# A Mamba-style vision block: one state's product with C on GpSimd in unit 10, and six issue places shifted

## The chip, the core and the metric

The kernel runs on one core of a Trainium2 chip. The metric is the device time of one execution in microseconds (us). The engines are named as in the profile: PE (matrix products; PEld is its weight load), DVE (VectorE), ACT (ScalarE), POOL (GpSimd) and SP, whose queue issues the DMAs.

## What is computed

Two images of 96 channels and 128 x 128 pixels pass through two layers. The first layer's mixer is four selective scans (rows, rows reversed, columns, columns reversed) over 16,384 positions. Each has 192 inner channels and 16 states:

```python
xc = silu(conv(xc) + conv_b)                       # causal, 4 taps
dt_raw, Bm, Cm = split(xc @ xproj_w.T)             # 6, 16, 16
dt = softplus(dt_raw @ dt_w.T + dt_b)
def step(h, t):
    dt_t, u_t, B_t, C_t = t
    dA = exp(dt_t[:, :, None] * A)
    h = dA * h + dt_t[:, :, None] * B_t[:, None, :] * u_t[:, :, None]
    y = einsum('bds,bs->bd', h, C_t)
    return (h, y)
y = (scan(step) + Dp * xc) * silu(z)
out = y @ outp_w.T
```

The four results are fused by one matrix and added to the input. After it come a normalised feed-forward network with quantised products, a 3 x 3 convolution in the second layer and another such network.

## The kernel before

For each image `normalize` makes the normalised input, `mamba` does the four scans, and `ffn_and_conv` does the rest. The change is in `mamba`, which takes most of the time.

`mamba` runs 64 **steps** for an image: 2 pairs of directions (row and column direction side by side on the 128 partitions, the second pair reversed) times 32 tiles of T = 512 positions. For two images that is 128 steps. The 2 x 192 channels of a pair make three groups g of 128 partitions. A step has 24 **units**, `units = [(g, s) ...]`, s = 0, 2, ... 14: a unit is two states of one group. Unit 8g + s/2 is (g, s), so unit 10 is (1, 4).

For a unit the work goes through the engines thus:

- SP loads the B row and the C row of four states, broadcast over partitions (`row_tile`, L346, tiles `row0` and `row1`, 1 MB each, 5 and 4 buffers). One such tile serves two units.
- POOL multiplies the B rows of two units by dt x u (`b_part`, L350) and adds the carried state into the first column (L354; L353 once for each group).
- ACT makes the decays exp(dt x A) into the PSUM tile `da` (`decay`, two L360 for a unit, 3 buffers).
- DVE scans the two states (`scan`, L364). In most units the result overwrites `da`. In the six units in `BY_POOL` (units 0, 4, 8, 12, 16, 20) it overwrites the B row tile instead.
- The product with C (h x c into the C row tile) is done by DVE (L459), or for the six units by POOL (`by_pool`, L371).
- ACT copies the last column of the state (L460) to `hst`, for the next step.
- PE sums the products over the states into the PSUM tile `y` with an identity matrix (`sums`, L368), starting each group from Dp x xc (L465). After a group's 8 units DVE multiplies y by the gate (`gated`, L375).

The order in each engine's queue is the order of the Python calls, written out by hand (`in_order`); nothing reorders it. The loop at the end of `mamba` goes over units k. At even k it issues B products for units k + 2 and k + 3. Then come `issue(k, 0)`, the first scan of unit k, `behind(k - 1)` (product with C, copy and sums of the unit before), the decay of unit k + 2, the second scan, `issue(k, 1)`. Where unit k - 1 is the first of a group, `behind` comes after the second scan. A POOL product of unit k is issued at (k + 1, 1), its sums at (k + 3, 1).

`issue(k, where)` hands out what `later` has put down for that unit. Besides the POOL products this is the preparation of the **next** step, `prologue`, whose list `at` holds (unit, where, function): `conv` and `conv_out` (the four taps on PE, evicted by ACT), `silu` of xc and of the gate sz (L270, with a load of the function table ahead, and L271, the load of the table for exp behind), `gate` and `gate_out` (PE, and the eviction by ACT, L258), `mix` (two DMAs that reorder rows of group 1), `rows` and `rows_out` (the projections), `rows_to_dram`, `dt_in` and `dt_out` (PE L295, ACT L300), `softplus` (L304, L305) and `dt_u` (POOL L309), `entry`. Units 24 and up are units of the step that uses the results: 27 is its unit 3. All matmul results of the preparation share one PSUM buffer, `misc`.

Of the kernel before, what the change touches and what calls it, by code (L numbers as in the profile page):

```python
# [15 lines left out]
ALU = mybir.AluOpType  # L16
# [7 lines left out]
T = 512  # L24
# [10 lines left out]
ROW_BUFS = (5, 4)  # L35
AHEAD = 2
BY_POOL = tuple((g, s) for g in range(3) for s in (0, 8))
BCO = 32
SEG = 8
NBC = 4 * S  # L40
# [3 lines left out]
def tile_metaformer(ctx: ExitStack, tc: tile.TileContext, a: dict, out: bass.AP):  # L44
    nc = tc.nc
# [5 lines left out]
    def const(name, shape):  # L51
        t = cpool.tile(list(shape), F32, name=name)
        nc.sync.dma_start(t, a[name])
        return t
# [20 lines left out]
    convb = const("convb", (128, 2, NG))  # L75
    bcw = const("bcw", (128, 2, NG, BCO + NBC))
    dtw = const("dtw", (2 * RK, 2, NG * 128))
# [113 lines left out]
    def mamba(acc, xnr, xnc, pools, heads):  # L191

        with ExitStack() as st:
            pool = lambda n, bufs, **kw: st.enter_context(tc.tile_pool(name=n, bufs=bufs, **kw))
# [6 lines left out]
            hst = one.tile([128, NG, S], F32, name="hst")  # L201
# [19 lines left out]
            def prologue(pi, i, d):  # L221

                rev = pi == 1
                first = pi == 0 and i == 0
                queue = nc.scalar if first else nc.sync
                lo = L - (i + 1) * T if rev else i * T
# [46 lines left out]
                def rows():  # L273

                    d["ps"] = misc()
                    for g in range(NG):
                        nc.tensor.matmul(  # L277
                            d["ps"][0 : BCO + NBC, :], bcw[:, pi, g, :], d["xc"][:, g, :], start=g == 0, stop=g == NG - 1
                        )

                def rows_out():
                    d["rows"] = one.tile([BCO + NBC, T], F32, name="rows")
                    nc.scalar.copy(d["rows"], d["ps"][0 : BCO + NBC, :])

                def rows_to_dram():

                    d["bcd"] = rows_d.tile([2, S // 4, 2, 4, T], F32, name="bcd")
                    queue.dma_start(d["bcd"].rearrange("k q d s t -> (k q d s) t"), d["rows"][BCO:, :])

# [25 lines left out]

                at = [(-3, 1, load), (3, 0, partial(mix, "xc")), (11, 0, partial(silu, "xc"))]
                at += [(25 if first else 9, 0, partial(mix, "sz")), (31, 1, partial(silu, "sz"))]
                at += [(12, 0, rows), (13, 1, rows_out), (14, 0, rows_to_dram)]  # L320
                for g, k in ((1, 1), (0, 5), (2, 9)):
                    at += [(k, 0, partial(conv, g)), (k + 1, 1, partial(conv_out, g))]
                gates = ((1, 24, 24, 1), (0, 27, 27, 1), (2, 28, 28, 1)) if first else ((1, 7, 8, 0), (0, 18, 19, 0), (2, 21, 22, 0))
                for g, k, o, where in gates:
                    at += [(k, 0, partial(gate, g)), (o, where, partial(gate_out, g))]
                soft = ((0, 1, 16), (1, 3, 26)) if first else ((0, 3, 17),)
                for x0, x1, k in soft:
                    at += [(k, 1, partial(softplus, x0, x1))]
                for g, k in enumerate((14, 24, 25) if first else (14, 15, 16)):
                    at += [(k, 0, partial(dt_in, g)), (k + 1, 0, partial(dt_out, g))]  # L330
                for g, k in enumerate((19, 27, 29)):
                    at += [(k, 0, partial(dt_u, g))]
                    if i > 0:
                        at += [((20, 24, 29)[g], 1, partial(entry, g))]

                outs = (conv_out, gate_out, rows_out, dt_out)
                at = [(k, where, getattr(f, "func", f) not in outs, f) for k, where, f in at]
# [23 lines left out]
                return da  # L361

            def scan(j, da, b, h):
                nc.vector.tensor_tensor_scan(h[:, j, :], da[:, j, :], b[:, j, :], 0.0, ALU.mult, ALU.add)  # L364

            def sums(s, y, c):
                for j in range(2):
                    nc.tensor.matmul(y, ident, c[:, j, :], start=False, stop=s + j == S - 1)  # L368

            def by_pool(h, c):  # L370
                nc.gpsimd.tensor_tensor(c, h, c, ALU.mult)  # L371

            def gated(pi, d, g, y):
                t = d["sz"][:, g, :]
                nc.vector.tensor_tensor(t, y, t, ALU.mult)  # L375
                d["yg"].append(t[:, ::-1] if pi == 1 else t)
# [24 lines left out]
            def later(k, where, rank, f, *args):  # L401
                todo.setdefault((k, where), []).append((rank, partial(f, *args)))

            def issue(k, where):
                for _, f in sorted(todo.pop((k, where), ()), key=lambda p: p[0]):
                    f()

            for k, where, rank, f in prologue(*steps[0], state[0]):
                if k < nu:
                    f()  # L410
                else:
                    later(k - nu, where, rank, f)

            def prepare(n):
                if n < len(steps):
                    for m, where, rank, f in prologue(*steps[n], state[n]):
                        k = (n - 1) * nu + m
                        if k < 0:
                            f()
                        else:  # L420
                            later(k, where, rank, f)

            prepare(1)
            bs, cs, das, hs, quads = {}, {}, {}, {}, {}

            def fetch(k, n, m):
                if k < total:
                    t = row_tile(state[k // nu], *units[k % nu], n)
                    m[k], m[k + 1] = t[:, 0:2, :], t[:, 2:4, :]
                    if n == 0:  # L430
                        quads[k] = t

            def feed(k):

                if k < total:
                    n = k // nu
                    b_part(steps[n][1], state[n], *units[k % nu], quads.pop(k))

            def feed_decay(k):
                if k < total:  # L440
                    n = k // nu
                    das[k] = decay(steps[n][0], state[n], *units[k % nu])

            ys = {}

            def gate_before(k):
                pn, pu = divmod(k - 1, nu)
                gated(steps[pn][0], state[pn], units[pu][0], ys.pop(k - 1))

            def begins(k):  # L450
                return 0 <= k < total and units[k % nu][1] == 0 and units[k % nu] in BY_POOL

            def behind(k):

                n, u = divmod(k, nu)
                (pi, i), d, (g, s) = steps[n], state[n], units[u]
                h, c = hs.pop(k), cs.pop(k)
                if (g, s) not in BY_POOL:
                    nc.vector.tensor_tensor(c, h, c, ALU.mult)  # L459
                nc.scalar.copy(hst[:, g, s : s + 2], h[:, :, T - 1])  # L460
                if s == 0:
                    if k > 0:
                        gate_before(k)
                    y = ps_y.tile([128, T], F32, name="y")
                    nc.tensor.matmul(y, dmat[:, pi, g, :], d["xc"][:, g, :], start=True, stop=False)  # L465
                else:
                    y = ys.pop(k - 1)
                ys[k] = y
                if (g, s) in BY_POOL:
                    later(k + 1, 1, True, by_pool, h, c)  # L470
                    later(k + 3, 1, True, sums, s, y, c)
                else:
                    sums(s, y, c)
                if k == total - 1:
                    gated(pi, d, g, y)
                if s == S - 2 and g > 0:
                    later(k + 4, 0, True, project, pi, i, d, g)
                    later(k + 5, 1, False, collect, pi, d, g)
# [7 lines left out]
            for k in range(total + 6):  # L486
                n, u = divmod(k, nu)
                if u == nu - 3:

                    prepare(n + 2)  # L490
                if k % 2 == 0:
                    fetch(k + 2 * B_AHEAD, 0, bs)
                    feed(k + AHEAD)
                issue(k, 0)
                if k < total:
                    (g, s) = units[u]
                    da, b = das.pop(k), bs.pop(k)
                    hs[k] = b if (g, s) in BY_POOL else da
                    scan(0, da, b, hs[k])
                if 0 < k <= total and not begins(k - 1):  # L500
                    behind(k - 1)
                feed_decay(k + AHEAD)
                if k < total:
                    scan(1, da, b, hs[k])
                if begins(k - 1):
                    behind(k - 1)
                if k % 2 == 0:
                    fetch(k + 2 * C_AHEAD, 1, cs)
                issue(k, 1)
# [160 lines left out]
def _layout(v):  # L670
# [9 lines left out]
    xw = v["L0_conv_xproj_w"]  # L680
    bcw = np.zeros((2, 2 * DI, BCO + NBC), f)
    dtw = np.zeros((2 * RK, 2, 2 * DI), f)
# [56 lines left out]
```

## Time and profile before

| | us |
|---|---|
| median of 3 runs (11122.3 to 11125.68) | 11124.08 |
| the profiled execution, its own time | 11117.1 |
| its span, first to last instruction | 11115.3 |

| engine | busy us | share of the span | instructions |
|---|---|---|---|
| PE | 10236.7 | 92% | 24592 |
| DVE | 10503.8 | 94% | 10337 |
| ACT | 7900.1 | 71% | 13564 |
| POOL | 9804.3 | 88% | 4908 |

Mean times of one instruction: L364 1216 ns into `da` and 1206 ns into a row tile, L459 1204 ns, L375 680 ns (DVE); L350 4526 ns, L371 2352 ns, L309 1271 ns, L354 200 ns (POOL); L360 691 ns, a table load 1283 ns, a Silu or Softplus of a whole step 1484 ns (ACT).

A line of the timeline gives start, length, engine, source line, operation, output and inputs; "x2" merges two that follow each other, and a bracket names idle time ahead of it and what seems to have ended it. The granted clock of PE is 0.994 over the span. In the table of windows the slices of the two scans are alike; the light slices in the middle and at the end are normalisation, networks and convolution.

### The profile page before, as it was taken

Reading aid. Unit: us, or ns where it says so; the run is one execution under the profiler, and the core shown is the slowest. Engines: PE = TensorE matmul, PEld = TensorE weight load, DVE = VectorE, ACT = ScalarE, POOL = GpSimd, SP = SyncE. Lnnn points to the kernel's source line nnn. Section 1 sums busy time; section 2 is a strip of 40 time slices with the busy share of each in tenths; the row PEclk is TensorE's granted clock in tenths of the full one; section 3 lists DMA queues with packets and bytes.
Section 4 is the critical chain, followed back from the end, with each engine's and each line's share of the span. In section 5 each row is a group of like instructions: output and inputs, shape, how many; then the busy total and the mean of one; then the engine's idle time right before and its main releaser. Section 6 shows DMA issues by size and latency. Waiting matters only on the chain.

```text
span 11115.3 us, 94135 instructions
## 1 busy us (share of the span) xinstructions
PE 10236.7 (92%) x24592; PEld 3996.3 (36%) x24592; DVE 10503.8 (94%) x10337; ACT 7900.1 (71%) x13564; POOL 9804.3 (88%) x4908
## 2 busy tenths in 40 slices
PE   8999999999999999998989999999999999999989
PEld 3333333333333333334433333333333333333344
DVE  7999999999999999996679999999999999999965
ACT  6777777777777777776677777777777777777766
POOL 6999999999999999993369999999999999999932
PEclk9999999999999999999999999999999999999999
DMA  8888888888888888881178888888888888888810
GB/s 306 340 339 336 344 339 340 339 336 343 339 342 336 341 340 339 343 331 70 28 282 344 336 338 343 338 342 337 338 343 339 341 338 336 344 340 340 336 53 16
DMA packets 540496, 3416.18 MB, mean 307 GB/s; under 512 B 67468, under 2 KB 68588, under 8 KB 143576
## 3 DMA queue, kind: packets, MB, share of 16 engines
q1 hardware_dynamic: 539160, 3408.84, 78.1%
q8 instruction: 199, 3.26, 0.1%
q14 instruction: 337, 2.76, 0.1%
q10 hardware_dynamic: 800, 1.31, 0.0%
HBM read 3288.26 MB, written 54.53 MB: 301 GB/s over the span
## 4 chain that ended last, share of the span: by engine, by line
DVE 56%; issue 19%; PE 12%; ACT 10%; POOL 3%; DMA 0%; DVEq 0%; SPq 0%; POOLq 0%; ACTq 0%
DVE da L364 34%; DVE row L364 11%; DVE row L459 9%; PE y L368 4%; ACT da L360 3%; POOL row L371 3%; PE pc L620 3%; PE v L130 2%; PE xm L124 2%; ACT sz L270 2%; ACT L270 2%; ACT L271 2%; PE ph L579 1%; DVE sz L375 1%; ACT mix L258 1%
## 5 line engine op out<-in xcount | busy, mean ns | idle before, releaser
L350 POOL TENSOR_TENSOR row<-dtu,row 128x2048 f32<-128x2048 f32 x1536 | 6951.6, 4526 | 7.6 <-DMA row<-bcd 7.1
L368 PE MATMUL y<-row,ident 128*128 128x512 f32 x12288 | 5682.0, 602 | 369.1 <-DVE row L459 356.5
L364 DVE TENSOR_TENSOR_SCAN da<-da,row 128x512 f32<-128x512 f32 x4608 | 5499.8, 1216 | 78.5 <-POOL row L371 23.0
L360 ACT ACTIVATE da<-dt,amat 128x512 f32<-128x512 f32 x6144 | 4234.6, 691 | 177.0 <-DVE row L364 4.5
L368 PEld LDWEIGHTS y<-row,ident 128*128 128x128 f32 x12288 | 2249.7, 190 | 3676.8 <-issue 2261.8
L459 DVE TENSOR_TENSOR row<-da,row 128x1024 f32<-128x1024 f32 x2304 | 2775.1, 1204 | 0.0
L371 POOL TENSOR_TENSOR row<-row,row 128x1024 f32<-128x1024 f32 x768 | 1806.7, 2352 | 268.2 <-issue 145.9
L460 ACT COPY hst<-da 128x2 f32<-128x2 f32 x2304 | 369.4, 160 | 2295.0 <-DVE row L459 2292.1
L364 DVE TENSOR_TENSOR_SCAN row<-da,row 128x512 f32<-128x512 f32 x1536 | 1852.5, 1206 | 34.7 <-DMA row<-bcd 32.4
L218 PE MATMUL misc<-xa,inx 96*64 96x512 f32 (+1 forms) x2048 | 935.0, 599 | 14.0 <-ACT dt L300 7.2
L218 PE MATMUL misc<-xb,inx 96*64 96x512 f32 (+1 forms) x2048 | 935.0, 599 | 1.6 <-ACT xc L250 1.6
L309 POOL TENSOR_TENSOR dtu<-dt,xc 128x512 f32<-128x512 f32 x384 | 488.0, 1271 | 188.9 <-ACT dt L304 102.6
L604 POOL TENSOR_TENSOR acc<-acc,y 96x512 f32<-96x512 f32 x128 | 147.4, 1151 | 526.5 <-DVE y L603 460.8
L383 PE MATMUL misc<-acc,ident 96*96 96x512 f32 x512 | 388.2, 843 | 218.5 <-ACT hst L460 196.4
L218 PEld LDWEIGHTS misc<-xa,inx 96*64 96x64 f32 (+1 forms) x2048 | 323.9, 163 | 580.8 <-issue 472.9
L465 PE MATMUL y<-xc,dmat 128*128 128x512 f32 x768 | 419.6, 628 | 110.6 <-DVE sz L375 110.6
L295 PE MATMUL misc<-rows,dtw 12*128 12x512 f32 x768 | 434.0, 645 | 59.2 <-ACT dt L300 34.4
L385 PE MATMUL misc<-sz,gmat 128*96 128x512 f32 x1024 | 483.6, 594 | 0.0
L620 PE MATMUL pc<-seg,uw 96*96 96x256 f32 x1536 | 419.2, 379 | 0.0
L218 PEld LDWEIGHTS misc<-xb,inx 96*64 96x64 f32 (+1 forms) x2048 | 323.4, 163 | 252.1 <-issue 187.2
L354 POOL TENSOR_TENSOR row<-row,enter 128x4 f32<-128x4 f32 x1488 | 298.2, 200 | 116.5
L277 PE MATMUL misc<-xc,bcw 128*96 128x512 f32 x768 | 355.8, 600 | 7.1 <-ACT xc L270 7.1
(92 smaller groups left out, 7402.7 us busy)
## 6 DMA issues: line engine op xcount, KB each, us to landing
row<-bcd SPq DMA_DIRECT2D x3072, 1024.0 KB, 7.5
xc<-mix SPq DMA_DIRECT2D x252, 128.0 KB, 4.7
sz<-mix SPq DMA_DIRECT2D x252, 128.0 KB, 4.8
xa<-xnr SPq DMA_DIRECT2D x124, 193.1 KB, 5.1
xb<-xnc SPq DMA_DIRECT2D x124, 193.1 KB, 5.5
bcd<-rows SPq DMA_DIRECT2D x126, 128.0 KB, 4.3
acc<-in_x_dram SPq DMA_DIRECT2D x16, 768.0 KB, 5.8
xnr<-xn SPq DMA_DIRECT2D x16, 768.0 KB, 4.3
```

The source lines that it names most:

```text
L218: nc.tensor.matmul(ps[rows, :], w(PAIRS[pi][d], k, lo, hi), src[d][:, k : k + T], **se)
L270: nc.scalar.activation(d[name], d[name], AF.Silu)
L295: nc.tensor.matmul(d["ps"], w, d["rows"][0 : 2 * RK, :], start=True, stop=True)
L309: nc.gpsimd.tensor_tensor(dtu, d["dt"][:, g, :], d["xc"][:, g, :], ALU.mult)
L350: nc.gpsimd.tensor_tensor(b, d["dtu"][g][:, None, :].broadcast_to((128, 4, T)), b, ALU.mult)
L360: nc.scalar.activation(da[:, j, :], d["dt"][:, g, :], AF.Exp, scale=amat[:, pi, g, s + j : s + j + 1])
L364: nc.vector.tensor_tensor_scan(h[:, j, :], da[:, j, :], b[:, j, :], 0.0, ALU.mult, ALU.add)
L368: nc.tensor.matmul(y, ident, c[:, j, :], start=False, stop=s + j == S - 1)
L371: nc.gpsimd.tensor_tensor(c, h, c, ALU.mult)
L385: nc.tensor.matmul(d["po"], gmat[:, pi, 2 * g - 2 + k, :], d["yg"][g - 1 + k], start=False, stop=k == 1)
L459: nc.vector.tensor_tensor(c, h, c, ALU.mult)
L620: nc.tensor.matmul(pc[:, k, :], uw[:, k0 + k, ky, :], rows, start=ky == 0, stop=ky == 2)
```

## The change

POOL does the product with C for state 0 of unit 10, and DVE that for state 1. The scan of state 0 in that unit writes the B row tile, that of state 1 `da`. The state copy of unit 10 becomes two copies, and its sums are issued in two parts: state 1 in `behind(10)`, state 0 at (13, 1). The POOL part is issued at (11, 1). Six entries in the list `at` change their place (those of the Silu and of `dt_u` for every step, the others for every step but an image's first, which has places of its own):

| entry | before | after |
|---|---|---|
| Silu of xc | 11, 0 | 11, 1 |
| `gate_out` of group 1 | 8, 0 | 8, 1 |
| `dt_in`, `dt_out` of group 2 | 16 and 17 | 17 and 18 |
| Softplus | 17, 1 | 18, 1 |
| `dt_u` of group 0 | 19 | 20 |
| `dt_u` of group 2 | 29 | 35 |

```diff
+HALF_POOL = ((1, 4),)
...
-                at = [(-3, 1, load), (3, 0, partial(mix, "xc")), (11, 0, partial(silu, "xc"))]
+                at = [(-3, 1, load), (3, 0, partial(mix, "xc")), (11, 1, partial(silu, "xc"))]
...
-                gates = ((1, 24, 24, 1), (0, 27, 27, 1), (2, 28, 28, 1)) if first else ((1, 7, 8, 0), (0, 18, 19, 0), (2, 21, 22, 0))
+                gates = ((1, 24, 24, 1), (0, 27, 27, 1), (2, 28, 28, 1)) if first else ((1, 7, 8, 1), (0, 18, 19, 0), (2, 21, 22, 0))
...
-                soft = ((0, 1, 16), (1, 3, 26)) if first else ((0, 3, 17),)
+                soft = ((0, 1, 16), (1, 3, 26)) if first else ((0, 3, 18),)
...
-                for g, k in enumerate((14, 24, 25) if first else (14, 15, 16)):
+                for g, k in enumerate((14, 24, 25) if first else (14, 15, 17)):
...
-                for g, k in enumerate((19, 27, 29)):
+                for g, k in enumerate((20, 27, 35)):
...
-                nc.vector.tensor_tensor_scan(h[:, j, :], da[:, j, :], b[:, j, :], 0.0, ALU.mult, ALU.add)
+                nc.vector.tensor_tensor_scan(h[j], da[:, j, :], b[:, j, :], 0.0, ALU.mult, ALU.add)
...
+            def product(engine, h, c, states):
+                if len(states) == 2:
+                    engine.tensor_tensor(c, h, c, ALU.mult)
+                for j in states if len(states) == 1 else ():
+                    engine.tensor_tensor(c[:, j, :], h[:, j, :], c[:, j, :], ALU.mult)
...
+            def by_pool(g, s):
+                return (0, 1) if (g, s) in BY_POOL else (0,) if (g, s) in HALF_POOL else ()
...
-                h, c = hs.pop(k), cs.pop(k)
-                if (g, s) not in BY_POOL:
-                    nc.vector.tensor_tensor(c, h, c, ALU.mult)
-                nc.scalar.copy(hst[:, g, s : s + 2], h[:, :, T - 1])
+                (da, b), c = hs.pop(k), cs.pop(k)
+                pool = by_pool(g, s)
+                rest = tuple(j for j in (0, 1) if j not in pool)
+                if rest:
+                    product(nc.vector, da, c, rest)
+                for h, states in ((b, pool), (da, rest)):
+                    if states:
+                        lo, hi = states[0], states[-1] + 1
+                        nc.scalar.copy(hst[:, g, s + lo : s + hi], h[:, lo:hi, T - 1])
...
-                if (g, s) in BY_POOL:
-                    later(k + 1, 1, True, by_pool, h, c)
-                    later(k + 3, 1, True, sums, s, y, c)
-                else:
-                    sums(s, y, c)
+                if pool:
+                    later(k + 1, 1, True, product, nc.gpsimd, b, c, pool)
+                    later(k + 3, 1, True, sums, s, y, c, pool)
+                if rest:
+                    sums(s, y, c, rest)
...
-                    hs[k] = b if (g, s) in BY_POOL else da
-                    scan(0, da, b, hs[k])
+                    hs[k] = da, b
+                    h = [(b if j in by_pool(g, s) else da)[:, j, :] for j in range(2)]
+                    scan(0, da, b, h)
```

More of the change, by code (lines that the diff above doesn't have):

```diff
@@ L363, in scan, with sums @@
             def scan(j, da, b, h):
-                nc.vector.tensor_tensor_scan(h[:, j, :], da[:, j, :], b[:, j, :], 0.0, ALU.mult, ALU.add)
-            def sums(s, y, c):
-                for j in range(2):
+                nc.vector.tensor_tensor_scan(h[j], da[:, j, :], b[:, j, :], 0.0, ALU.mult, ALU.add)
+            def sums(s, y, c, states=(0, 1)):
+                for j in states:
                     nc.tensor.matmul(y, ident, c[:, j, :], start=False, stop=s + j == S - 1)
-            def by_pool(h, c):
-                nc.gpsimd.tensor_tensor(c, h, c, ALU.mult)
+            def product(engine, h, c, states):
[3 more added lines that the diff above has]
+                    engine.tensor_tensor(c[:, j, :], h[:, j, :], c[:, j, :], ALU.mult)
             def gated(pi, d, g, y):
@@ L503, in mamba @@
                 if k < total:
-                    scan(1, da, b, hs[k])
+                    scan(1, da, b, h)
                 if begins(k - 1):
```

## The prediction

> **What bounds the kernel now.** I read the table of windows first, to see which engine has room where, then the timelines of the engines over one step, and last the groups, for the price of one instruction.
>
> ```profile
> 1000.00:5000.00 4000.00, 3708.75 (x8566) 1407.79 (x8565) 3969.21 (x3570) 2880.94 (x4963) 3844.39 (x1851) 1.00 0.86 339
> ```
>
> After the window's length stand PE, PEld, DVE, ACT and POOL busy, then clock, DMA share and GB/s. In the scan DVE is busy 99.2% of the time, POOL 96.1%, PE 92.7%, ACT 72.0%. The chain of waits for the whole run gives DVE 56% and POOL 3%. So DVE sets the pace, POOL is next, and little on DVE is idle. The gating product L375 runs three times a step: 155 of them start between 1017.7 and 4987.2 us, so a step lasts 3969.5 / 154 x 3 = 77.33 us, and 128 steps are 9898 us of the span.
>
> ```profile
> 2071.74 2.47 DVE L364 TENSOR_TENSOR_SCAN da<-da,row 128x512 f32<-128x512 f32 x2
> 2074.24 0.69 DVE L375 TENSOR_TENSOR sz<-y,sz 128x512 f32<-128x512 f32 x1
> 2075.16 1.23 DVE L364 TENSOR_TENSOR_SCAN da<-da,row 128x512 f32<-128x512 f32 x1 [0.23 <-POOL row L371]
> ...
> 2084.14 1.22 DVE L364 TENSOR_TENSOR_SCAN row<-da,row 128x512 f32<-128x512 f32 x1
> 2085.50 3.61 DVE L364 TENSOR_TENSOR_SCAN da<-da,row 128x512 f32<-128x512 f32 x3
> ```
>
> This is DVE at units 9, 10, 12 and 13 of one step. Records overlap a little, so I price an instruction by start to next start: elsewhere in this timeline a scan takes 1.12, a product L459 1.12, L375 0.59. Two places break that. Unit 10's first scan comes 0.92 after L375, 0.33 too late. Unit 13's comes 1.36 after the scan before it, 0.24 too late. The first is put down to POOL's L371, but that instruction makes nothing this scan reads. ScalarE shows the cause of both:
>
> ```profile
> 2069.00 1.28 ACT L270 ACT_TABLE_LOAD   x1
> 2070.30 1.48 ACT L270 ACTIVATE sz<-sz 128x1536 f32<-128x1536 f32 x1
> 2071.80 1.28 ACT L271 ACT_TABLE_LOAD   x1
> 2073.09 0.59 ACT L258 COPY mix<-misc 128x512 f32<-128x512 f32 x1
> 2073.57 0.17 ACT L460 COPY hst<-da 128x2 f32<-128x2 f32 x1
> 2073.62 2.76 ACT L360 ACTIVATE da<-dt,amat 128x512 f32<-128x512 f32 x4
> ...
> 2079.08 0.67 ACT L250 ACTIVATE xc<-misc,convb 128x512 f32<-128x512 f32 x1
> 2079.77 1.28 ACT L270 ACT_TABLE_LOAD   x1
> 2081.06 1.49 ACT L270 ACTIVATE xc<-xc 128x1536 f32<-128x1536 f32 x1
> 2082.56 1.28 ACT L271 ACT_TABLE_LOAD   x1
> 2083.86 0.16 ACT L460 COPY hst<-da 128x2 f32<-128x2 f32 x1
> 2084.05 1.42 ACT L360 ACTIVATE da<-dt,amat 128x512 f32<-128x512 f32 x2
> ```
>
> A Silu with its two table loads is a burst of 4.09 us (2079.77 to 2083.86), in which no decay (L360) is made. Unit 10's decay ends near 2075.06, unit 13's at 2085.47; each scan starts right behind it. The decay, not POOL, is the releaser.
>
> ```profile
> 2072.70 2.36 POOL L371 TENSOR_TENSOR row<-row,row 128x1024 f32<-128x1024 f32 x1
> 2075.02 4.53 POOL L350 TENSOR_TENSOR row<-dtu,row 128x2048 f32<-128x2048 f32 x1
> 2079.63 0.20 POOL L354 TENSOR_TENSOR row<-row,enter 128x4 f32<-128x4 f32 x1
> ...
> 2085.49 2.35 POOL L371 TENSOR_TENSOR row<-row,row 128x1024 f32<-128x1024 f32 x1 [0.90 <-PE y L368]
> ```
>
> POOL's room is what it waits ahead of its C products. They start 1.35 us after the start of the second scan of their unit (2084.14 to 2085.49), so they wait for DVE. In this step that is 0.90 (unit 12), 0.68 (unit 16) and 0.43 (unit 0), 2.01 us in all.
>
> **The change, part by part.** All per step, then times 128.
>
> *The product on DVE.* In unit 10 L459 (1.12) becomes a product over 128x512. No such product is in the trace; the bounds are 0.56 (half of L459) and 1.12 (no saving). I take 0.59, L375's spacing, since it has the same sizes and also reads one operand from a PSUM tile. That is -0.53. The first scan of unit 10 now writes a row tile: 1.11 against 1.12, -0.01.
>
> *The product on POOL.* 128x512 from row tiles: between 1.16 (half of 2.31, L371's spacing) and 1.24 (L309, of this size). I take 1.24. POOL's work is 12 B products of 4.76 (L350 start to the one behind L354), 3 L353 at 0.16 more, 6 C products of 2.31, 3 dt x u of 1.23: 75.15. With the new one it is 76.39, still under DVE's 77.33, so it is paid from the 2.01 of waits.
>
> [...]
>
> *The gate's eviction* (L258, 8,0 to 8,1) goes behind unit 7's state copy and unit 10's decay on ACT. That decay starts about 0.5 earlier, at about 2073.1, and is done by 2074.6, before the scan's natural 2074.83: -0.33. Behind the eviction wait PE's convolution of group 2 (1.2 to 1.4 later; its result is not taken up before the next decay, at 2078.75) and on SP the two sz DMAs, about 1.4 later, with B and C rows behind them. A row lands in 7.5 us and is taken up 12 or more us after its issue, so this is hidden; with that lead gone it would cost up to 1.4.
>
> *The Silu of xc* (11,0 to 11,1) goes past unit 10's copies and unit 13's decay. Unit 13's stall goes: -0.24. Late next is unit 14's decay. Let T be the start of unit 10's half product on DVE. Its copy starts at T+0.72, unit 13's decay at 0.91, and from there 1.43 for the pair, 4.09 burst, 0.19 copy of unit 11: unit 14's decay starts at 6.62, ends 8.04; scan possible at 8.08. DVE gets there at T+0.59+4x1.12+1.25+1.12 = T+7.44 (a scan straight behind its unit's first one takes 0.13 more, as in the 2.47 above). New stall +0.64. Bounds: 0 if ACT is ready, 4.09 if nothing hides the burst. The second copy of unit 10's state (0.18) falls in the time before the half product ends. PE's `rows` matmuls wait for the Silu, some 1.8 us, hidden under PE's 291 idle us in 4000 (5.6 a step).
>
> *Last dt product, its eviction and Softplus* (16 to 17, 17 to 18, 17,1 to 18,1). The matmul passes unit 15's sums, the eviction unit 19's decay. Softplus, 4.09 again, passes unit 17's copy and unit 20's decay. From the start of unit 17's product: copy 1.24, decay 1.43, 5.52 to the gate eviction, 0.47 to the copy, 0.19, 1.42: unit 21's decay done at 9.03 where its scan comes at 8.95: +0.12 with the signal. Today the Softplus holds up unit 20's decay with 1.3 to spare, so nothing is won. Bounds 0 and 0.5.
>
> *Two dt x u on POOL.* Group 0's goes behind one B product, and Softplus' values are there about 3 us before. Group 2's leaves its place ahead of unit 4's C product and goes ahead of the half product: POOL reaches units 4 and 8 earlier and becomes late at unit 12. Following POOL's order with DVE's new times, unit 14's B is ready 1.1 us before its scan and unit 16's 0.57 before. Nothing is paid while that 0.57 lasts.
>
> Sum: -0.53 -0.01 -0.33 -0.24 +0.64 +0.12 = -0.35, a step of 76.98. Times 128: -44.8 us. The profiled run took 11117.1 (span 11115.3), so 11072.3; the median of the three runs, 11124.1, is 7 higher, which gives 11,079.
>
> **The rivals.**
>
> *POOL becomes the bound, slower.* Its place is unit 16's B rows, its point 0.57: from a half product of 1.81 on, B is late there. If POOL keeps its three waits of 2.01 on top of 76.39, the step is 78.40, +1.07, and the time 11124 + 137 = 11,261. For it: POOL has 0.94 us left in a step of 77.33, and the half product waits for more than L371 does. Against: those waits are for DVE, and shrink as POOL falls behind.
>
> *The stall moves and eats all.* If unit 14's scan waits 1.0 instead of 0.64, the rest is cancelled: 11,124. For it: ACT does the same work, only later, and unit 14 is next to unit 13. Against: the decay is a fixed row, and 0.35 more would have to come from somewhere.
>
> *ACT is ready in time.* If both new stalls vanish, POOL's 76.39 bounds: -0.94 x 128 = -120, 11,004. For it: POOL would then be seen without waits. Against: the burst of 4.09 has only to fit one gap, and by the rows doesn't.
>
> **How the numbers follow.** Forecast 0.62, with its own range 11,045 to 11,110 (unit 14's stall 0.25 either way); POOL bound 0.17; stall eats all 0.06; ACT ready 0.15. A measurement here can tell about 0.2%, 22 us. Faster by more: 0.58 of the forecast (0.04 of it lies above 11,102) and 0.15, so 0.73; within 0.10; slower 0.17. Range 11,030 to 11,125: it takes in the forecast, the second rival and half of the third.
>
> **What would show it.** Right: L375 spacings that sum to 77.0 a step; the unit 10 gap of 0.23 gone from DVE; no gap at unit 13 but one of about 0.64 at unit 14, behind a decay that starts where L271 ends; L371's waits down from 2.0 to under 1. Wrong: DVE waiting for L350 or L354 at unit 16 (POOL bound), a half product on DVE near 1.1, on POOL above 1.8, or the unit 14 gap near 1.

## The result and the profile after

| | before | after |
|---|---|---|
| median, us (6 runs each, same chip) | 11121.53 | 11384.39 |
| span of the profiled execution, us | 11115.3 | 11383.1 |
| granted clock of PE over the span | 0.994 | 0.97 |
| a step, us (spacing of the gating product, 1000 to 5000 us) | 77.33 | 79.5 |

The changed kernel is slower: ratio 1.0237, interval 1.0224 to 1.025, 263 us. The forecast was 11,079 and the range ended at 11,125. The time is lost in the steps: 2.19 us in each (3975.7 us for 150 spacings, three to a step), which over all 128 would be 280, near the 263 measured.

In the new file the lines have moved: the scan is L365, the decay L361, both products with C L373 (DVE and POOL), the half products L375, the sums L369, the gating product L379, the state copy L472, the gate's eviction L259, Softplus L305 and L306, the table load behind a Silu L272, `project` L387 and L389, a group's opening matmuls L477.

First the table of windows for the same stretch as in the prediction (length, then PE, PEld, DVE, ACT, POOL busy, clock, DMA share, GB/s), after the change:

```profile
1000.00:5000.00 4000.00, 3678.38 (x8355) 1412.62 (x8354) 3842.84 (x3473) 2820.93 (x4878) 3798.07 (x1849) 0.97 0.84 330
```

DVE's busy time fell from 3969 to 3843: the engine that set the pace now stands idle for 157 us in 4000 (31 before), about 3.1 in each step. PE's clock fell from 1.00 to 0.97. The table of waits for the same stretch (engine, tile and line, the releaser it names, us in total, times, longest) says who stands:

```profile
PE misc L387 <- ACT hst L472: 208.8, 48, 4.4
ACT sz L259 <- PE misc L219: 197.1, 50, 4.4
DVE row L365 <- ACT hst L472: 115.8, 50, 3.1
```

Each of the three occurs about once a step, and the last one, 2.3 us a time, is DVE's loss. To see how they hang together, ACT's timeline in one step:

```profile
2077.07 1.28 ACT L305 ACT_TABLE_LOAD   x1
2078.36 1.48 ACT L305 ACTIVATE dt<-dt 128x1536 f32<-128x1536 f32 x1
2079.86 1.28 ACT L306 ACT_TABLE_LOAD   x1
2081.16 0.59 ACT L259 COPY sz<-misc 128x512 f32<-128x512 f32 x1
...
2092.26 0.59 ACT L259 COPY sz<-misc 128x512 f32<-128x512 f32 x1 [3.73 <-PE misc L219]
```

The same eviction before the change, in another step (there it is L258, behind the Softplus' second table load, L305):

```profile
2103.43 1.28 ACT L305 ACT_TABLE_LOAD   x1
...
2106.27 0.58 ACT L258 COPY sz<-misc 128x512 f32<-128x512 f32 x1
```

PE's timeline after the change, in the step of the first view:

```profile
2075.46 1.98 PE L369 MATMUL y<-row,ident 128*128 128x512 f32 x4 [0.26 <-DVE row L373]
2081.80 2.02 PE L387 MATMUL misc<-acc,ident 96*96 96x512 f32 x2 [4.35 <-ACT hst L472]
2083.61 2.60 PE L389 MATMUL misc<-sz,gmat 128*96 128x512 f32 x4
...
2091.19 1.02 PE L219 MATMUL misc<-xb,inz 96*128 96x512 f32 x2
```

`project` before the change, behind the eviction of 2106.27:

```profile
2106.90 1.10 PE L383 MATMUL misc<-acc,ident 96*96 96x512 f32 x2 [1.56 <-ACT hst L460]
2107.83 1.88 PE L385 MATMUL misc<-sz,gmat 128*96 128x512 f32 x4
```

Two windows of the changed step, at PE's pause and behind it:

```profile
2077.00:2082.00 5.00, 0.65 (x3) 0.20 (x2) 5.00 (x5) 4.91 (x7) 4.92 (x3) 0.96 0.91 385
2082.00:2085.00 3.00, 3.00 (x4) 1.04 (x5) 2.94 (x4) 2.69 (x5) 2.92 (x4) 0.50 0.01 3
```

And DVE's one long wait in it:

```profile
2094.45 1.22 DVE L365 TENSOR_TENSOR_SCAN row<-da,row 128x512 f32<-128x512 f32 x1 [1.94 <-ACT hst L472]
```

Read together: Softplus and its two table loads (2077.07 to 2081.16) now stand directly ahead of the eviction of group 0's gate (L259). Before, the burst was over at 2104.71, a copy and a decay earlier than that eviction. The eviction empties the one `misc` buffer, which the next user in PE's queue, `project`, must have. So PE stands from 2077.44 to 2081.80, although the view names the state copy as the releaser: the matmul starts 0.05 us after the eviction's end (2081.75), and the copy L472 ends later, at 2081.81. Behind the pause the clock is 0.50, and `project` goes from 2081.80 to 2086.21, 4.41 us, where before the change the same six matmuls took 2.81 (2106.90 to 2109.71). PE is then late with the sums and with the gate of group 2 (2091.19). ACT, in order too, waits 3.73 us for that gate, with the decays behind it, and DVE's first scan of unit 0 waits 1.94 for its decay.

Stretches of PE clock at 0.50 in the trace's clock record, 1000 to 5000 us: one before the change (6.8 us), 50 after it (221.9 us in all), one in every step. Of these 35 last 3.41 us and 15 last 6.83.

What the prediction had said of units 10 and 14 can be read here as well. DVE's timeline after, units 9 to 10 and 13 to 14:

```profile
2046.89 0.69 DVE L379 TENSOR_TENSOR sz<-y,sz 128x512 f32<-128x512 f32 x1
2047.49 1.21 DVE L365 TENSOR_TENSOR_SCAN row<-da,row 128x512 f32<-128x512 f32 x1
...
2057.06 2.47 DVE L365 TENSOR_TENSOR_SCAN da<-da,row 128x512 f32<-128x512 f32 x2
2059.99 1.23 DVE L365 TENSOR_TENSOR_SCAN da<-da,row 128x512 f32<-128x512 f32 x1 [0.45 <-ACT da L361]
```

Unit 10's scan comes 0.60 after the gating product, so its stall is gone. Unit 14's first scan comes 2.93 after the start of a pair that is worth 2.37 (1.25 + 1.12): a stall of 0.56 where the prediction had 0.64.

### The profile page after: what moved, and what is told of

It is laid out like the page before. It is cut to its first block, busy times and chain, and to the rows that moved or that the text cites. A ratio compares the mean times of both kernels' runs of the same rounds, so it can differ in the third digit from the quotient of the medians.

```text
span 11383.1 us, 95023 instructions
## 1 busy us (share of the span) xinstructions
PE 10402.7 (91%) x24592; PEld 4100.4 (36%) x24592; DVE 10457.8 (92%) x10337; ACT 7935.4 (70%) x13692; POOL 9953.2 (87%) x5036
## 3 DMA queue, kind: packets, MB, share of 16 engines
q14 instruction: 344, 2.82, 0.1%
## 4 chain that ended last, share of the span: by engine, by line
DVE 48%; PE 20%; ACT 18%; issue 13%; POOL 1%; DMA 0%; DVEq 0%; POOLq 0%; SPq 0%; ACTq 0%
DVE da L365 25%; DVE row L365 12%; DVE row L373 7%; ACT da L361 6%; PE y L369 6%; PE misc L389 3%; PE pc L633 2%; DVE sz L379 2%; PE v L131 2%; PE misc L387 2%; PE xm L125 2%; ACT xc L271 2%; ACT dt L305 2%; ACT L271 1%; ACT L272 1%
## 5 line engine op out<-in xcount | busy, mean ns | idle before, releaser
L351 POOL TENSOR_TENSOR row<-dtu,row 128x2048 f32<-128x2048 f32 x1536 | 6952.4, 4527 | 9.2 <-DMA row<-bcd 8.4
L369 PE MATMUL y<-row,ident 128*128 128x512 f32 x12288 | 5591.4, 599 | 56.9 <-DVE row L373 56.0
L365 DVE TENSOR_TENSOR_SCAN da<-da,row 128x512 f32<-128x512 f32 x4480 | 5359.6, 1216 | 106.4 <-ACT da L361 60.5
L361 ACT ACTIVATE da<-dt,amat 128x512 f32<-128x512 f32 x6144 | 4234.6, 691 | 173.2 <-DVE row L365 3.7
L369 PEld LDWEIGHTS y<-row,ident 128*128 128x128 f32 x12288 | 2312.6, 192 | 3236.6 <-issue 2579.3
L373 DVE TENSOR_TENSOR row<-da,row 128x1024 f32<-128x1024 f32 x2176 | 2618.0, 1203 | 0.0
L365 DVE TENSOR_TENSOR_SCAN row<-da,row 128x512 f32<-128x512 f32 x1664 | 2009.6, 1208 | 323.3 <-ACT hst L472 287.7
L373 POOL TENSOR_TENSOR row<-row,row 128x1024 f32<-128x1024 f32 x768 | 1807.2, 2353 | 389.4 <-PE y L369 227.3
L472 ACT COPY hst<-da 128x2 f32<-128x2 f32 (+1 forms) x2304 | 369.0, 160 | 1942.7 <-DVE row L373 1887.2
L387 PE MATMUL misc<-acc,ident 96*96 96x512 f32 x512 | 464.3, 1000 | 548.7 <-ACT hst L472 513.3
L389 PE MATMUL misc<-sz,gmat 128*96 128x512 f32 x1024 | 658.5, 778 | 0.0
L259 ACT COPY sz<-misc 128x512 f32<-128x512 f32 x256 | 150.1, 586 | 496.9 <-PE misc L219 495.4
L477 PE MATMUL y<-xc,dmat 128*128 128x512 f32 x768 | 419.2, 627 | 43.9 <-DVE sz L379 43.9
```

The costliest lines, as they stand in the source:

```text
L351: nc.gpsimd.tensor_tensor(b, d["dtu"][g][:, None, :].broadcast_to((128, 4, T)), b, ALU.mult)
L361: nc.scalar.activation(da[:, j, :], d["dt"][:, g, :], AF.Exp, scale=amat[:, pi, g, s + j : s + j + 1])
L365: nc.vector.tensor_tensor_scan(h[j], da[:, j, :], b[:, j, :], 0.0, ALU.mult, ALU.add)
L373: engine.tensor_tensor(c, h, c, ALU.mult)
L387: nc.tensor.matmul(d["po"], ident[0:C, 0:C], d["acc"], start=True, stop=False)
L389: nc.tensor.matmul(d["po"], gmat[:, pi, 2 * g - 2 + k, :], d["yg"][g - 1 + k], start=False, stop=k == 1)
```

## The experiments

Each kernel was compared with the kernel before on the same chip; the medians of that were 11119.28, 11119.46 and 11122.5 us in the three groups (names e1, e2, e3). The diffs below that change a tuple such as `gates` or `soft` change places in the list `at`; they are cut to the part that changes.

**1. The eviction ahead of Softplus** (e1_gate_first), otherwise the changed kernel:

```diff
-gates = ... ((1, 7, 8, 1), (0, 18, 19, 0), (2, 21, 22, 0))
+gates = ... ((1, 7, 8, 1), (0, 18, 18, 1), (2, 21, 22, 0))
```

> The changed kernel with one eviction (group 0's gate, L259) issued ahead of the Softplus instead of behind it; Softplus stays where the change put it. Theory A (PE idles behind the Softplus, because its next product needs the one misc buffer that this eviction frees): PE's idle time before L387, 4.35 us in a step, falls under 1, the clock stays at 1.0, the wait of unit 0's first scan goes, and the time falls to 11040 to 11100, about the blind forecast. Theory B (POOL or ACT is the bound, the Softplus only stands near it): 11330 to 11400, no real change.

Measured: 11066.58 us, ratio 0.9955 (0.994 to 0.9969), clock 0.99. This one place is worth 318 us against the changed kernel, and the result is 0.5% faster than the kernel before. ACT's timeline, then PE's:

```profile
2094.26 0.58 ACT L259 COPY sz<-misc 128x512 f32<-128x512 f32 x1
2094.85 1.28 ACT L305 ACT_TABLE_LOAD   x1
```

```profile
2094.89 1.10 PE L387 MATMUL misc<-acc,ident 96*96 96x512 f32 x2 [0.17 <-ACT sz L259]
```

PE waits 0.17 instead of 4.35, and the view names the eviction itself. 156 gating products from 1012.5 to 4988.3 us make a step of 3975.8 / 155 x 3 = 76.95 us; the forecast was 76.98. The clock isn't quite at the 1.0 that was expected: ten half-clock stretches of 3.41 us are left in the 4000. Eight of them begin within 0.7 us behind a pause of 1.5 to 1.6 us. An example, in which the clock record has 0.50 from 1644.26 on:

```profile
1643.69 6.50 PE L369 MATMUL y<-row,ident 128*128 128x512 f32 x10 [1.50 <-DVE row L373]
```

**2. PE kept busy in the pause** (e1_pe_filled): the changed kernel with four matmuls of a zero matrix into y ahead of `project`. They add nothing to the result and leave the eviction where it was.

```diff
+                if g == 1 and i > 0:
+                    y = list(ys.values())[-1]
+                    for _ in range(4):
+                        nc.tensor.matmul(y, zero, d["xc"][:, 0, :], start=False, stop=False)
```

> The changed kernel with four matmuls of a zero matrix, added into y, issued on PE ahead of the projection of groups 0 and 1, where PE idles 4.35 us. Theory A1 (part of the loss is the lower granted clock after the idle time: 0.70 for some 5 us, L387 and L389 take 1.6 to 2.6 us more): they run at full speed again, the granted clock is back near 0.99, and the time falls by 100 to 250 us although PE does more. Theory A2 (only the idle time itself counts): within 40 us of 11384.

Measured: 11134.13 us, 1.0015 (1.0005 to 1.0024), clock 0.992, two half-clock stretches in 4000 us, one of them behind a pause of 4.35 in the first step of a pair, which the edit leaves empty. PE's timeline (L391 is the filling):

```profile
2107.50 3.60 PE L391 MATMUL y<-xc,zero 128*128 128x512 f32 x8
2112.01 1.10 PE L393 MATMUL misc<-acc,ident 96*96 96x512 f32 x2 [0.91 <-ACT hst L478]
```

More work makes it 250 us faster. `project` starts as late as before, but takes 2.82 us (2112.01 to 2114.83), close to the 2.81 before the change, and not 4.41. So 250 of the 318 us are the clock. The other 68 remain with the late start; of these the table of waits shows unit 0's scan waiting 20.0 us in 4000, 0.39 a step, which is 50 us over 128.

**3. One and two zero matmuls** (e2_fill_1, e3_fill_2): the same with `range(1)` and `range(2)`.

> As e1_pe_filled (11134.1), but one matmul of the zero matrix instead of four, so that PE idles some 3.5 us of the 4.35. If the clock drops only after an idle time longer than that: near 11134, 11110 to 11160, granted clock 0.99. If any idle time of some us lowers it: 11300 to 11390, granted clock 0.97. Between the two: it drops in a part of the steps.

> As e1_pe_filled and e2_fill_1, with two matmuls of the zero matrix: PE should idle about 2.6 us before the projection. If the clock drops only after an idle time between 2.6 and 3.5 us: 11110 to 11160, granted clock 0.99. If the limit lies between 0.9 and 2.6 us: 11300 to 11390, clock 0.97.

Measured: one, 11386.44 us, 1.0242 (1.0225 to 1.0259), PE still idle for 3.49 us, 50 half-clock stretches of 221.9 us, as in the changed kernel: no help. Two, 11343.08, 1.0197 (1.018 to 1.0214), 47 stretches. PE's timeline with two:

```profile
2077.39 2.02 PE L393 MATMUL misc<-acc,ident 96*96 96x512 f32 x2 [2.63 <-ACT hst L478]
```

With a pause of 2.63 us in one piece the clock still fell to 0.50 in nearly every step (47 stretches in 4000 us); with one of 0.91 (four matmuls) there are two stretches, and none of the 52 pauses of 1.56 ahead of `project` in the kernel before has one behind it. The ends of matmuls are modelled; from weight load to weight load the same pauses are 3.46, 1.74 and 2.39.

The length of a pause alone doesn't settle it, though. In experiment 1, of the 52 pauses of 1.5 to 1.6 us in 4000 only eight were followed by a drop. What sets those eight apart no run shows.

**4. Softplus and the dt product back at their old places** (e1_softplus_back), the rest as changed:

```diff
-soft = ... ((0, 3, 18),)
+soft = ... ((0, 3, 17),)
...
-for g, k in enumerate(... (14, 15, 17)):
+for g, k in enumerate(... (14, 15, 16)):
```

> The changed kernel with the last dt product, its eviction and the Softplus at their old places; the half product, the Silu, the gate's eviction and the two dt x u at the new ones. Theory A: 11030 to 11090, the stall of 0.12 at unit 21 is gone too. Theory B: 11330 to 11400.

Measured: 11133.91 us, 1.0014 (1.0005 to 1.0024), clock 0.992. The clock came back, so the move of Softplus and the dt product was what had lowered it; but the time missed its 11,030 to 11,090. The table of waits, 1000 to 5000 us:

```profile
DVE sz L379 <- PE y L369: 31.7, 52, 0.6
```

That is 0.61 a step, 78 us over 128, on a wait that the changed kernel doesn't have. With the Silu later, the rows and then the dt products come later on PE, and with dt_in of group 2 back ahead of unit 15's sums these are too late for the gating product. The Silu's move is not enough for that: with it alone (experiment 8) the gating product has no wait. It takes the earlier DVE of the rest of the set as well. So the dt move, by which the prediction said that "nothing is won", is needed in this set; that it is the dt product's place and not Softplus' follows from PE's order, no run moved the two apart. The sum comes out: 11,067 - 15 (unit 21's stall, by the prediction) + 78 = 11,130.

**5. Only Softplus and the dt product moved** (e1_softplus_alone): the kernel before with the two edits of experiment 4 the other way round.

> The kernel before with only the last dt product, its eviction and the Softplus at their new places. Theory A: slower by 220 to 300 us, 11340 to 11420, with PE idle over 4 us before the projection of groups 0 and 1 (L383). Theory B (the loss needs the half product on POOL): within 40 us of the kernel before.

Measured: 11468.7 us, 1.0316 (1.0301 to 1.0331), clock 0.957, 74 half-clock stretches of 334.5 us. Alone the move costs 349 us, more than the 220 to 300 expected, and has 24 half-clock stretches more than the changed kernel. PE's pause was over 4 us in half of the steps only, and 3.2 in the others. POOL's part of the waits:

```profile
POOL dtu L309 <- ACT dt L304: 125.5, 50, 2.7
```

Group 0's dt x u is still at unit 19 here, and POOL stands 2.5 us a step for Softplus. The move to 20, which the prediction priced at nothing, goes with it. How much of the excess is this wait and how much the clock, no run separates.

**6. No half product** (e2_no_half): experiment 1 with `HALF_POOL = ()`.

> As e1_gate_first (11066.6), but DVE makes the whole product of unit 10 again; all moves stay. Theory H (DVE is the chain, the half product is worth its 0.53 + 0.01 us in each of 128 steps): 11066.6 + 69, so 11125 to 11145. Theory N (POOL or ACT sets the step, DVE's 0.53 is slack): 11055 to 11075.

Measured: 11133.87 us, 1.0015 (1.0006 to 1.0024). Against experiment 1 the half product on POOL is worth 67 us, 0.53 a step. DVE stands idle for 38 us in 4000 in both, so the difference is DVE's own work. The moves without it cost 14 us; the prediction's terms for them add up to -0.33 - 0.24 + 0.64 + 0.12 = +0.19, 24 us.

**7. Only the half product** (e3_half_alone): the changed kernel with all six places back.

> The kernel before with the half product on POOL and none of the moves. By the terms of the prediction DVE saves 0.54, but the Silu's burst in front of unit 13's decay doesn't get shorter and the second state copy (0.18) stands behind it, so unit 13's stall grows from 0.24 to about 0.95: net +0.2 a step, 11125 to 11160. A rival in which the half product alone brings its 0.54: 11045 to 11065.

Measured: 11264.72 us, 1.0129 (1.0114 to 1.0144), clock 0.978: a miss, 100 us above what was expected. Unit 13's stall grew, as foreseen, from 0.24 to about 0.9 (idle 0.77 in the timeline). But the waits and the windows show more:

```profile
DVE sz L379 <- PE y L369: 51.8, 31, 2.8
```

```profile
2121.50:2125.00 3.50, 3.50 (x5) 1.06 (x4) 3.50 (x4) 2.29 (x5) 3.42 (x4) 0.51 1.01 404
```

In 31 of the 51 steps the gating product waits for PE, and in the step shown the clock is halved just ahead of that. PE's timeline there:

```profile
2119.76 1.12 PE L296 MATMUL misc<-rows,dtw 12*128 12x512 f32 x2 [0.56 <-ACT rows L284]
2121.19 3.49 PE L369 MATMUL y<-row,ident 128*128 128x512 f32 x4 [0.31 <-DVE row L373]
```

No pause is long. PE waits for the rows, which the stall made late, and for a product, and has only the dt product (1.12 us) in between. The run has 31 half-clock stretches (139.9 us in the same 4000); what lowers the clock behind waits as short as these no run shows. So without the moves PE loses more than the half product brings: half product alone +142, moves alone +14, both -53 (the last two with the eviction in front).

**8. Only the gate's eviction of group 1 moved** (e2_gate_only) **and only the Silu moved** (e2_silu_only), each in the kernel before:

```diff
-gates = ... ((1, 7, 8, 0), ...
+gates = ... ((1, 7, 8, 1), ...
```

```diff
-(11, 0, partial(silu, "xc"))
+(11, 1, partial(silu, "xc"))
```

> The kernel before with only the eviction of group 1's gate behind unit 10's decay. Decay theory (the 0.33 stall at unit 10's first scan waits for the decay behind that eviction): 11119 - 42, so 11070 to 11090, and no gap at unit 10. POOL theory (the stall waits for L371, as the profile's releaser says): no change, 11110 to 11130.

> The kernel before with only the Silu of xc behind unit 13's decay. By the terms of the prediction, -0.24 + 0.64 a step: 11150 to 11185. If the later Silu also holds up the dt chain, as the 0.62 us wait of unit 17's gating product on PE in e1_softplus_back suggests, up to 0.6 more: 11185 to 11270. A rival in which the Silu's place doesn't matter alone: 11110 to 11130.

Measured: eviction 11091.0, 0.9974 (0.9964 to 0.9983), 28 us; Silu 11177.16, 1.0051 (1.0036 to 1.0066), 58 us slower. The first settles the prediction's reading of unit 10: with POOL untouched the gap is gone, so L371, which the view named, was not the releaser. The gain is 0.22 a step, not 0.33. PE's waits:

```profile
PE misc L218 <- ACT mix L258: 51.5, 51, 1.0
```

Group 2's convolution now waits 1.0 for this eviction, the Silu behind it starts later, and unit 13's stall grows. The prediction had named this wait, and given the cover as the next decay; the Silu stands behind that. The Silu alone was worth -0.24 + 0.64 = +0.40 by the prediction, 51 us, and the longer hold-up of the dt chain that the expectation allowed for did not show.

**9. Group 2's dt x u back** (e3_dtu2_back), 35 to 29 in experiment 1:

```diff
-for g, k in enumerate((20, 27, 35)):
+for g, k in enumerate((20, 27, 29)):
```

> As e1_gate_first (11066.6) with group 2's dt x u back at its place ahead of unit 4's C product. The prediction paid nothing for that move while POOL has room: 11055 to 11080. If POOL's order bounds the step: above 11090.

Measured: 11068.43, 0.9954 (0.9939 to 0.9969), the same as experiment 1. This move carries nothing that can be measured.

## Why the prediction was wrong

**The step that failed** is the one on Softplus. It said: "Softplus, 4.09 again, passes unit 17's copy and unit 20's decay", priced what DVE loses by it at unit 21 (+0.12, bounds 0 and 0.5), and stopped there. The same list has "5.52 to the gate eviction": the eviction of group 0's gate was seen, and seen to be behind Softplus, but only as time that passes ahead of the decay. Nobody was named who waits for it. For the other eviction the prediction did ask that, and named PE's convolution. Here the answer was `project`, through the single `misc` buffer: PE stands 4.35 us in place of 1.56; the 2.8 between them had no price. Experiment 1 gives this omission 318 us. The 0.12 that was priced, 15 us, was right: in experiment 1 unit 21's first scan starts 1.26 behind the scan before it, 0.14 late.

**The second half of the same step**: the prediction had PE's room as "291 idle us in 4000 (5.6 a step)", said of the Silu, and took idle time of PE as free. A pause 2.8 us longer would have fitted that sum. The runs show two prices. Behind the pause of 4.35 us the clock was 0.50 for 3.41 or 6.83 us in every step (250 us, experiment 2), and even at a clock of 0.992 (experiment 2) PE comes late with group 2's gate, for which ACT's decays wait in order (the 68 us that are left, of which the waits show 50). The pause of 1.56 before the change had no such stretch behind it; with the one of 2.63 left by two zero matmuls (3.46 from one weight load's end to the next one's start) there were 47 in some 50 steps. Experiments 1 and 7 have stretches behind shorter pauses (1.5 to 1.6 and 0.56 us between matmuls, 2.3 and 1.4 between weight loads), so these runs give no one length from which the clock falls. No rival had this mechanism: the one on the slow side put the cost on POOL.

**What held.** With the eviction in front the step is 76.95 (forecast 76.98) and the time 53 us under before (forecast 45). In detail: the half product on DVE is 0.59 from start to next start (2069.26 to 2069.85 in experiment 1), as taken. POOL's takes 1.23, taken as 1.24. Unit 10's stall is gone and unit 13's too (the scans of 2074.34 there follow one another). Unit 14's stall is 0.55 (2.92 less 2.37), taken as 0.64. Unit 10's part was overpriced when it stands alone (0.22 against 0.33), not in the set, where unit 13's stall goes as well.

**The rivals.** POOL as the bound fell: in experiment 1 POOL waits ahead of its C products for 25 us in 4000, 0.5 a step (107.6 before, 2.1 a step), no scan of DVE waits for L351, and taking a POOL move back changed nothing. "ACT ready in time" fell with unit 14's stall in every run that moves the Silu. "The stall eats all" gave 11,124, and the stall was smaller than the forecast, not larger. The changed kernel took none of these ways.

**What to look for** was listed for DVE, POOL and the decays only. In the changed kernel the unit 10 gap, the unit 14 stall and POOL's half product are as predicted, and the step is 2.5 us longer than forecast all the same. One listed sign did fail with it: POOL's waits ahead of its C products rose to 3.1 us a step (155 in 4000) instead of falling under 1. But none pointed at the cause; a line on PE's waits and clock was missing.

## What to carry to other kernels

When a burst is moved on an in-order engine, list everything behind it in that queue, and for each the next user of the buffer that it frees; what feeds the bounding engine directly is only one of them. The sum of an engine's idle time says nothing of what one longer pause costs (here 2.8 us more of it in each step went with 318 us): price a pause by what it can do to the clock and by what waits behind it. And a set of moves is not the sum of its parts: here the half product costs 142 us without the moves, the moves cost 14 without the half product, and together, with one eviction put in front, they give 53.

## What the runs showed of the hardware

In the changed kernel 50 half-clock stretches, at 0.50, lasted 3.41 us (35 of them) or 6.83 (15). With a PE pause recorded as 2.63 us in a step there were 47 of them in some 50 steps; of 52 pauses of 1.5 to 1.6 us in experiment 1 only eight had one behind them, and the kernel before had 52 of 1.56 ahead of `project` without any. The half product alone had 31 (139.9 us); in the step shown PE's waits ahead were 0.56 and 0.31 us. Eight useless matmul instructions (four in the program) in the pause made the whole kernel 250 us faster. The releaser that the view names can be wrong in the same way twice: a state copy stood for the eviction just ahead of it, and POOL for a decay. The cause both times was the instruction whose result or buffer was needed and whose end lay 0.05 to 0.10 us ahead of the start.
